# Normalising two row tiles one block product later in a masked attention kernel with a hand-written ScalarE order

## The chip, the core and the metric

The kernel runs on one core of a Trainium2 chip. The core has a matrix engine (TensorE, PE in the profile), a vector engine (VectorE, DVE), an engine for activations and copies (ScalarE, ACT), GpSimd (POOL), and SyncE (SP), which here only issues transfers. Each engine works through its own list of instructions in order and waits at semaphores for the others. The metric is the device time of one execution in microseconds; lower is better. Before the change three executions took 645.16, 645.79 and 647.13 us, median 645.79.

## The reference

One layer of graph attention over 2708 nodes with 1024 features, all in float32:

```
h   = relu(layernorm(x))
q,k,v = h@Wq.T+bq, h@Wk.T+bk, h@Wv.T+bv
z   = (q@k.T)/sqrt(1024) * adj          # adj is 0/1, about 0.15% ones
z   = where(z == 0, -10000, z)
out = x + relu(softmax(z) @ v)
```

A node has some four neighbours, so the kernel finds the few columns of each row of `adj` that are not zero, gathers those rows of `h`, and does the softmax over them alone.

## The kernel before

Rows are worked on in 22 tiles of 128. Wq and Wk are first joined into one matrix M, so that scores are products of `h@M` with gathered rows of `h`; Wv is applied after the softmax. The heavy work is therefore two multiplications of all row tiles by a 1024x1024 matrix. They are done for two tiles at a time (a unit): `("q", 0, 1)`, `("q", 2, 3)`, `("q", 4, 5)`, `("q", 6, 7)` and so on, and later `("o", ...)` units with Wv. A unit is cut into 2x2 blocks of 512 and takes seven block products instead of eight, so it needs sums of blocks of the rows (s1 to s4) and of the matrix (T). A block product is four calls, which the trace shows as eight matmuls of 128x512.

`multiply(n, ...)` writes out one unit. It holds three accumulator banks: X and Z, which start as copies of the bias row (`banks_for`, line 713), and Y, which starts as a copy of X after its first product (line 961). The first two products of the next unit, `a11` into its X and `s1` into its Z, are made inside the current one, by `between(n)`, ahead of the current unit's last product (`a22` into Y). Four banks are shared by all units, so the next unit's Z bank is the one that the current unit's X leaves when `c11` has copied it out (line 1026).

Between the products stand calls `after(i)`, i from 0 to 6. They do what lies beside the multiplication. First come the parts of the next unit: turning its rows with TensorE (line 402, eight transposes of 128x128 for a tile), copies and sums of blocks (lines 684 and 688), and at i = 3 the two bias copies. Then come the steps that the table `steps_at` names for (unit, i):

- `a6`: `apply(6)`, two ScalarE activations (line 263) that normalise the row tiles 6 and 7 in place;
- `k6`: `keep(6, False)`, which stores both to `h_dram` by two transfers from ScalarE's queue (line 270) and leaves their addition to `hsum` for later;
- `p13`, `p14`: `counted(k)`, one ScalarE pass over a tile of `adj` that counts its ones (line 355);
- `f`, `e`, `i`: `found`, four VectorE searches of an `adj` tile for its ones (line 376), and `listed`, which sorts out what was found for a batch of up to four tiles (lines 389 to 395).

The `adj` tiles come through three buffers, `adj_sb[0..2]`. A load into a buffer (line 347, SP's queue) waits until both the count on ScalarE and the search on VectorE have read what is in it.

Up to unit 4 the lists of ScalarE and VectorE stand exactly as the code is written (`manual_schedule`); GpSimd's list is written out for the first part as well. TensorE's and SP's lists are set by a scheduler that takes the data dependences into account. So a step that is moved in the table moves at once on ScalarE, and can move other work on TensorE and SP.

The place in question is in unit 1 (tiles 2 and 3), after its third product (i = 2) and after its fourth (i = 3). The rows of tiles 6 and 7 are named `x_941` and `x_943`; unit 3 turns and multiplies them. In unit 1 the banks are `ps_876` (X), `ps_878` (Z) and a `psy`; unit 2's are `ps_1079` and `ps_1081` before the change, and named `ps_1075` and `ps_1077` after it. Unit 3's X and Z are `ps_1256` and `ps_1258`, its sums `s_1241` (s1), `s_1245` (s2) and so on. The results of unit 1 are `q_990` and `q_991`, stored to `q_dram` from ScalarE's queue (line 1022) behind the copy of line 1037; those of unit 2, `q_1187` and `q_1188`, are stored from SP's queue.

Of the kernel before, what the change touches and what calls it, by code (L numbers as in the profile page):

```python
# [63 lines left out]
def tile_preln_masked_attention(  # L64
# [651 lines left out]
    def natural_rows(n):  # L716
# [16 lines left out]
    nc.vector.tensor_scalar(large[:, 1:2], large[:, 1:2], 250000.0 / D, None, op0=ALU.is_gt)  # L733

    steps_at = {(0, 0): "s4-5 p8 e9 +19 +20 +21", (0, 1): "r4 +0 +1 +2 i10.0-1", (0, 3): "p10", (0, 4): "i10.2-3 a4",
# [4 lines left out]
    steps_ahead = {(1, 5): "o1", (3, 6): "o0"}  # L740
# [740 lines left out]
```

## Time and profile before

| | |
|---|---|
| median of three executions | 645.79 us (645.16 to 647.13) |
| profiled execution | 646.32 us |
| its span, first to last instruction | 644.5 us |
| granted TensorE clock | 0.998 |
| TensorE busy | 636.8 us |
| VectorE busy | 521.3 us |
| GpSimd busy | 376.3 us |
| ScalarE busy | 279.8 us |
| HBM read and written | 159.81 MB, 42.31 MB |

The profile's views used here are: the page (totals by engine and costly groups), the list of waits (who waited for whom), the timeline (instructions in order, with the idle time ahead of each and what ended it in brackets), the chain of waits (the chain of work that ended last, followed back), tables by stretches of time, and the transfers by queue in a stretch. In the timeline an entry begins with its start and its length in us. A queue's name ends in q: `SPq` is SP issuing a transfer. Queue q1 of the transfers carries what SP issues, q10 what ScalarE issues, q0 what GpSimd issues.

### The profile page before, as it was taken

To read this page: it belongs to the slowest core of one execution; us is meant where nothing else is said; L and a number is where in the kernel's file an instruction comes from. 1 tells how busy PE (TensorE), PEld (TensorE's weight loads), DVE (VectorE), ACT (ScalarE), POOL (GpSimd) and SP (SyncE) were. 2 spreads that over 40 slices of the span, in tenths; PEclk is the share of its full clock that TensorE was granted. 3 is DMA by queue.
4 is the path that set the end of the run, shared out by engine and by line. 5 is a ranking of instruction groups with operands and counts; after the bars stand their busy time and mean duration, and the time that the engine had idled before them with its cause. 6 is when DMAs were issued, how large, how long until landed. Compare 5 with 4: busy or idle time off the path is not lost.

```text
span 644.5 us, 6383 instructions
## 1 busy us (share of the span) xinstructions
PE 636.8 (99%) x1731; PEld 326.5 (51%) x1731; DVE 521.3 (81%) x1014; ACT 279.8 (43%) x426; POOL 376.3 (58%) x400
## 2 busy tenths in 40 slices
PE   9999999999999999999999999999999999999996
PEld 5777766444444444445444444454544444545442
DVE  5999789888796765989878959987999999989121
ACT  3448984849586532323133132433333344333300
POOL 2649950975859457744734635565685856762431
PEclk9999999999999999999999999999999999999999
DMA  8999997598699969997877998988798989984542
GB/s 340 407 350 326 345 340 289 203 327 297 226 325 347 382 203 398 374 372 253 319 236 271 420 417 283 334 270 250 248 322 282 288 324 322 306 234 122 147 144 88
DMA packets 61986, 189.02 MB, mean 293 GB/s; under 512 B 10701, under 2 KB 11037, under 8 KB 61048
## 3 DMA queue, kind: packets, MB, share of 16 engines
q0 software_dynamic: 27888, 84.95, 41.1%
q1 hardware_dynamic: 29994, 89.36, 37.6%
q10 hardware_dynamic: 4062, 14.24, 5.7%
q8 instruction: 16, 0.26, 0.2%
q14 instruction: 26, 0.21, 0.1%
HBM read 159.81 MB, written 42.31 MB: 314 GB/s over the span
## 4 chain that ended last, share of the span: by engine, by line
PE 94%; DVE 3%; DMA 2%; issue 0%; POOL 0%; POOLq 0%; SPq 0%
PE ps L948 42%; PE psy L948 30%; PE ps_y L463 6%; PE pt L402 5%; PE ps_x L463 4%; PE ps_z L463 4%; DMA adj<-in_adj_dram 2%; DVE at L376 1%; PE ps_y L498 1%; DVE st L224 1%; PE ps_h L1153 0%; PE ps_v L581 0%; DVE cand L394 0%; DVE sort L668 0%; DVE y_alone L1297 0%
## 5 line engine op out<-in xcount | busy, mean ns | idle before, releaser
L597 POOL DMA_INDIRECT g<-h_dram,tab x105 | 124.4, 1184 | 70.4 <-issue 22.0
L948 PE MATMUL ps<-M,a 128*128 128x512 f32 x320 | 144.1, 593 | 0.6 <-ACT ps L713 0.6
L948 PE MATMUL psy<-wlow,s 128*128 128x512 f32 x320 | 143.9, 592 | 0.0
L826 DVE SCALAR_TENSOR_TENSOR junk<-g,pq 128x1024 uint8<-128x1024 f32 x93 | 114.1, 1227 | 8.3 <-DMA g<-h_dram,tab 5.9
L879 DVE SCALAR_TENSOR_TENSOR u<-g,coef,u 128x1024 f32<-128x1024 f32 x79 | 101.4, 1283 | 5.6 <-ACT u L871 3.7
L948 PEld LDWEIGHTS ps<-M,a 128*128 128x128 f32 x320 | 59.3, 190 | 69.0 <-issue 67.4
L948 PEld LDWEIGHTS psy<-wlow,s 128*128 128x128 f32 x320 | 59.2, 190 | 67.3 <-issue 66.5
L376 DVE FIND_INDEX8 at<-ones,adj 128x8 uint32<-128x685 f32 (+1 forms) x88 | 74.5, 865 | 0.0
L948 PE MATMUL ps<-wlow,s 128*128 128x512 f32 x160 | 72.0, 593 | 0.8 <-DVE s L688 0.8
L948 PE MATMUL psy<-wlow,a 128*128 128x512 f32 x160 | 72.2, 593 | 0.0
L948 PE MATMUL ps<-M,s 128*128 128x512 f32 x160 | 71.9, 592 | 0.0
L355 ACT ACTIVATE sized<-adj 128x2708 uint8<-128x2708 f32 (+1 forms) x22 | 54.2, 2465 | 9.4 <-DMA adj<-in_adj_dram 8.5
L285 POOL TENSOR_TENSOR hsum<-hsum,x 128x256 f32<-128x256 f32 (+1 forms) x56 | 38.7, 727 | 29.7 <-DVE wlow L431 22.2
L1047 POOL DMA_INDIRECT y<-in_x_dram,tab x19 | 32.8, 1726 | 32.5 <-ACT taken L1013 11.2
L948 PEld LDWEIGHTS ps<-wlow,s 128*128 128x128 f32 x160 | 30.3, 190 | 39.3 <-issue 36.4
L948 PEld LDWEIGHTS ps<-M,s 128*128 128x128 f32 x160 | 30.3, 190 | 38.1 <-issue 37.6
L948 PEld LDWEIGHTS psy<-wlow,a 128*128 128x128 f32 x160 | 30.3, 190 | 37.8 <-issue 37.3
L778 POOL DMA_INDIRECT out_dram<-y,tab x21 | 27.8, 1323 | 17.5 <-DMA y<-in_x_dram,tab 9.2
L688 DVE TENSOR_TENSOR s<-a,pt 128x512 f32<-128x512 f32 x40 | 25.6, 682 | 13.1 <-remote 5.9
L684 ACT COPY a<-pt 128x512 f32<-128x512 f32 x60 | 33.4, 589 | 4.6 <-PE psy L948 3.1
L597 POOL DMA_INDIRECT M<-h_dram,tab x20 | 24.9, 1243 | 13.9 <-ACT u L871 4.7
L871 ACT ACTIVATE u<-g,coef 128x1024 f32<-128x1024 f32 x16 | 18.4, 1148 | 25.2 <-DVE m L869 12.3
(238 smaller groups left out, 848.4 us busy)
## 6 DMA issues: line engine op xcount, KB each, us to landing
adj<-in_adj_dram SPq DMA_DIRECT2D x21, 1354.0 KB
x<-in_x_dram SPq DMA_DIRECT2D x21, 512.0 KB
h_dram<-x ACTq DMA_DIRECT2D x21, 512.0 KB
q_late<-q SPq DMA_DIRECT2D x12, 512.0 KB
pq<-q_late SPq DMA_DIRECT2D x12, 512.0 KB
u_dram<-u SPq DMA_DIRECT2D x10, 512.0 KB
or<-u_dram SPq DMA_DIRECT2D x10, 512.0 KB
g<-in_wv_dram SPq DMA_DIRECT2D x16, 256.0 KB
```

Source lines behind the costliest of these rows:

```text
L285: small.append(nc.gpsimd.tensor_add(hsum[:n, cols], hsum[:n, cols], xt[:n, cols]))
L355: nc.scalar.activation(sized[:n], a[:n, :, :PW], AF.Abs, accum_out=total[:n, t:t + 1])
L376: nc.vector.max_index(at[:n, k - first_k, g, :], ones[:n, 0:8], a[:n, g, :])
L402: nc.tensor.transpose(pt[:, c, :], xt[:, k * P:(k + 1) * P], ident)
L463: mm = nc.tensor.matmul(bank, a_tile(o + H * a[0], a[1], i), b(o), start=first and o == 0, stop=(o == H - 1), skip_group_check=True)
L597: return nc.gpsimd.indirect_dma_start(out=dst, out_offset=None, in_=src, in_offset=off, bounds_check=N - 1, oob_is_err=False)
L684: nc.scalar.copy(ops[name], bank)
L778: to = nc.gpsimd.indirect_dma_start(out=out, out_offset=bass.IndirectOffsetOnAxis(ap=ptab.bitcast(U32)[:n, t, SLOTS:SLOTS + 1], axis=0), i ...
L826: chained(lambda: nc.vector.scalar_tensor_tensor(junk, g_of[t][s], 1.0, tq[t], op0=ALU.mult, op1=ALU.mult, accum_out=zall[:, t, s:s + 1]))
L879: chained(lambda: nc.vector.scalar_tensor_tensor(u, g_of[t][s], coef[:, at[t][s]:at[t][s] + 1], u, op0=ALU.mult, op1=ALU.add))
L948: mm = nc.tensor.matmul(bank, a[:, c, :], b[:, c, :], start=False, stop=(c == 3), skip_group_check=True)
L1047: return nc.gpsimd.indirect_dma_start(out=y[:n], out_offset=None, in_=x, in_offset=off, compute_op=ALU.add)
```

## The change

The steps `a6 k6` are taken from place (1, 2) of the table and put at the head of place (1, 3):

```diff
-                (0, 5): "f11 p11 k4 s6-7", (0, 6): "+3 +4 f12 m6 m7", (1, 1): "p12 f13 c1 r6 +5", (1, 2): "p13 a6 k6",
-                (1, 3): "p14", (1, 5): "s8-10 w8-14 r8 w15-21 f14 f15", (1, 6): "f16 p15", (2, 1): "f17",
+                (0, 5): "f11 p11 k4 s6-7", (0, 6): "+3 +4 f12 m6 m7", (1, 1): "p12 f13 c1 r6 +5", (1, 2): "p13",
+                (1, 3): "a6 k6 p14", (1, 5): "s8-10 w8-14 r8 w15-21 f14 f15", (1, 6): "f16 p15", (2, 1): "f17",
```

On ScalarE, in unit 1 between the count of the last 20 rows of `adj` and the count `p14`, the order changes as follows (lines with + stand so after the change, lines with - before it):

```order
 L355 ACTIVATE sized,total<-adj_157 20x2708
+L1026 COPY q_990<-ps_876 128x512
+L713 COPY ps_1075<-bp_sb 128x512
+L713 COPY ps_1077<-bp_sb 128x512
 L263 ACTIVATE x_941<-x_941,r 128x1024
 L263 ACTIVATE x_943<-x_943,r 128x1024
 L270 DMA h_dram<-x_941 128x1024
 L270 DMA h_dram<-x_943 128x1024
-L1026 COPY q_990<-ps_876 128x512
-L713 COPY ps_1079<-bp_sb 128x512
-L713 COPY ps_1081<-bp_sb 128x512
```

The copy of unit 1's X and the two bias copies into unit 2's banks now stand ahead of the two activations and the two stores, instead of behind them.

On TensorE, at the end of unit 1, the scheduler has placed the turning of tile 6 differently:

```order
 L664 MATMUL ps_all<-sort,ones_h 128x252
+L948 MATMUL ps_1075<-M,a_997 128x512 x4
+L948 MATMUL ps_1077<-wlow,s_1060 128x512 x4
+L948 MATMUL psy<-wlow,a_892 128x512 x4
 L402 MATMUL pt<-ident,x_941 128x128 x8
-L948 MATMUL psy<-wlow,a_892 128x512
-L948 MATMUL ps_1079<-M,a_997 128x512 x4
-L948 MATMUL ps_1081<-wlow,s_1060 128x512 x4
-L948 MATMUL psy<-wlow,a_892 128x512 x3
 L948 MATMUL psy<-wlow,s_1064 128x512 x4
```

Before, the transposes of `x_941` and one of the four calls of unit 1's last product stood ahead of unit 2's first two products; now unit 2's two products come first, then unit 1's last product in one piece, and then the transposes.

On SP, one load of `adj` and one store of unit 2 change places, further down:

```order
 L347 DMA adj_155<-in_adj_dram 128x4x677
 L347 DMA adj_157<-in_adj_dram 128x4x677
+L347 DMA adj_159<-in_adj_dram 128x4x677
 L1022 DMA q_dram<-q_1187 128x1024
-L347 DMA adj_159<-in_adj_dram 128x4x677
 L347 DMA adj_155<-in_adj_dram 128x4x677
 L1022 DMA q_dram<-q_1188 128x1024
```

The load into the third `adj` buffer now stands ahead of the store of `q_1187`. VectorE's and GpSimd's lists are the same in both kernels.

## The prediction

> **What bounds the kernel now.** I read the page first, then the list of waits for TensorE, then the timeline around the moved steps, and last the chain of waits through that place.
>
> The page's span and engine totals:
>
> ```profile
> span 644.5 us, 6383 instructions
> PE 636.8 (99%) x1731; PEld 326.5 (51%) x1731; DVE 521.3 (81%) x1014; ACT 279.8 (43%) x426; POOL 376.3 (58%) x400
> ```
>
> TensorE is busy for all but 7.7 us. The list of all its waits (us in total, times, longest):
>
> ```profile
> PE ps_y L498 <- POOL hsum L112: 1.2, 1, 1.2
> PE ps L948 <- DVE s L688: 0.8, 1, 0.8
> PE ps L948 <- ACT ps L713: 0.6, 1, 0.6
> ```
>
> The first is the start of the program; what the list lacks of the 7.7 us, some 5, is the tail behind the last matmul. So two waits are left in the middle, and both lie near the change. Nothing that leaves the matmuls as they are can win much more than these two, while losses have no such bound. TensorE's timeline there (start, length, instruction, idle time before it):
>
> ```profile
> 144.23 3.60 PE L948 MATMUL ps<-M,a 128*128 128x512 f32 x8
> ...
> 154.76 1.04 PE L402 MATMUL pt<-ident,x 128*128 128x128 f32 x8
> 155.63 1.09 PE L948 MATMUL psy<-wlow,a 128*128 128x512 f32 x2
> 157.31 3.70 PE L948 MATMUL ps<-M,a 128*128 128x512 f32 x8 [0.59 <-ACT ps L713]
> 160.85 3.60 PE L948 MATMUL ps<-wlow,s 128*128 128x512 f32 x8
> 164.28 2.74 PE L948 MATMUL psy<-wlow,a 128*128 128x512 f32 x6
> 166.85 3.60 PE L948 MATMUL psy<-wlow,s 128*128 128x512 f32 x8
> ...
> 181.46 3.60 PE L948 MATMUL ps<-M,a 128*128 128x512 f32 x8
> 185.82 3.67 PE L948 MATMUL ps<-wlow,s 128*128 128x512 f32 x8 [0.76 <-DVE s L688]
> 189.33 3.60 PE L948 MATMUL psy<-wlow,a 128*128 128x512 f32 x8
> ```
>
> Ends are modelled, so I go by starts. A group of eight without a stall takes 3.43 us (160.85 to 164.28), that is 0.43 for one matmul, and the eight transposes 0.87 (154.76 to 155.63).
>
> Stall one: from 154.76 to 166.85 TensorE does eight transposes and 24 matmuls, 0.87 + 3 x 3.43 = 11.16 us of work in 12.09. It lost **0.93**.
>
> Stall two: from 181.46 to 189.33 stand two groups, 6.86 in 7.87. It lost **1.01**, waiting for VectorE's sum s1 of unit 3 (`s_1241`).
>
> **Stall one: what ScalarE does there.** ScalarE's timeline:
>
> ```profile
> 153.40 2.36 ACT L263 ACTIVATE x<-x,r 128x1024 f32<-128x1024 f32 x2
> 154.66 1.48 ACTq L270 DMA_DIRECT2D h_dram<-x  x2
> 156.18 0.59 ACT L1026 COPY q<-ps 128x512 f32<-128x512 f32 x1 [0.42 <-PE pt L402]
> 156.66 1.11 ACT L713 COPY ps<-bp_sb 128x512 f32<-128x512 f32 x2
> 167.06 0.59 ACT L1037 COPY q<-psy 128x512 f32<-128x512 f32 x1 [1.99 <-PE psy L948]
> 167.06 0.94 ACTq L1022 DMA_DIRECT2D q_dram<-q  x2
> ```
>
> The bank that `a_997` accumulates into is filled by the first copy of line 713, which stands behind two activations and the issue of two stores: from 153.40 to 156.18, 2.78 us. Those four are what moves. The copy of line 1026 needs the product into unit 1's X, the one at 144.23, so with the four out of the way it starts at 153.40, and the first bank is ready 2.78 earlier: TensorE could begin that group at 157.31 - 2.78 = 154.53. TensorE reaches it at 154.76, as it now stands right behind the small product `ps_all`. Margin 0.23; the whole 0.93 goes. Should the second bank copy hang on VectorE's last read in unit 1, which ends at 155.5 by the chain below, it still has until 154.76 + 3.43 = 158.19.
>
> **The four moved instructions in their new place.** The two activations follow at about 154.9 and end near 157.3, the stores are issued by 157.7, and the count `p14` starts then as before (both orders have the same sum). Three others wait for them. The copy that opens Y of unit 2 (line 961) stands behind `p14` and ends near 161; TensorE wants that bank for s2 at 154.76 + 3 x 3.43 + 0.87 = 165.92, 5 us later. The transposes of tile 6 come at 165.05, 8 us after its activation. The two stores to `h_dram` (0.52 MB each) are issued about 2.5 us later. What hides them is the quiet stretch of the transfer engines, in the table by stretches (busy time of each engine, clock, share of the transfer engines, GB/s):
>
> ```profile
> 163.00:167.00 4.00, 4.00 (x11) 1.85 (x10) 4.00 (x10) 0.59 (x1) 2.97 (x4) 1.00 0.07 14
> ```
>
> 0.07 busy for 4 us: a megabyte that slips 2.5 us runs into an empty stretch. Cost 0; without that cover, up to 2.6 us of delay for the load below.
>
> **Stall two: what is late there.** Taking 0.93 out ahead would by itself make TensorE wait 0.93 longer at 185.82, if `s_1241` comes no earlier. So the forecast hangs on what holds VectorE. The chain of waits through it:
>
> ```profile
> 154.85 0.69 DVE q L1029
> ...
> 162.98 3.39 DVE at L376 x4
> ...
> 166.43 10.14 DMA adj<-in_adj_dram
> ...
> 178.40 3.48 DVE at L376 x5
> ...
> 185.01 0.68 DVE s L688
> ```
>
> VectorE's last search of the batch waits for a load of `adj` issued at 166.43, by SP, when the buffer came free; the load takes 12 us until 178.40. VectorE had nothing to do from 173.08 on:
>
> ```profile
> 172.22 0.86 DVE L376 FIND_INDEX8 at<-ones,adj 128x8 uint32<-128x685 f32 x1
> 178.40 0.09 DVE L376 MATCH_VALUE_LOAD at<-ones,adj 128x8 f32 x1 [5.31 <-issue]
> ```
>
> Why 12 us for 1.39 MB (128 x 2708 x 4 bytes)? The transfers by queue (packets, MB, share), first row from 166.4 to 171, the next two from 171 to 175.7:
>
> ```profile
> q1 hardware_dynamic: 195, 0.53, 49.4%
> ...
> q10 hardware_dynamic: 259, 0.98, 53.5%
> q1 hardware_dynamic: 313, 0.84, 45.4%
> ```
>
> From 171 on, the load (q1) shares the engines half and half with the two stores of unit 1 (q10, 2 x 0.52 MB), issued at 167.06, just behind it. Now these stores move. They are issued with the copy of line 1037, which waits for unit 1's last product. That ended at 166.85 (the copy began 0.21 later); with the three groups in a row from 154.76 it ends at 165.05, so copy and first store come at 165.26, 1.17 **ahead** of the load, the second store 0.61 later. The load's own issue hangs on VectorE's searches since 154.85, behind a product ahead of the change, and stays at 166.43.
>
> What is a store worth that is issued ahead of the load? Behind the load, those of 167.06 moved nothing by 171 (no q10 in the first row). One that no load preceded closely is that of 183.26, with the q10 row from 184 to 185:
>
> ```profile
> 183.26 0.34 ACTq L270 DMA_DIRECT2D h_dram<-x  x1
> ...
> q10 hardware_dynamic: 89, 0.36, 91.8%
> ```
>
> It ran at full rate within 1 us. I take this case, as the engines are as empty at 165 as they were then. The stores then run from about 166.2, and 1.05 MB at the (0.98 + 0.84) / 4.7 = 0.39 MB/us of the shared rows end near 168.9, when the load begins to move. By 171 it has its 0.53 MB less at most 0.1; the other 0.9 to 1.0 take 2.5 us, to 173.5. The last confirmation came 178.40 - 175.7 = 2.7 later than the load's 1.39 MB were through; I keep between 0.3 and that, so 173.8 to 176.2, where VectorE has waited until 178.40. `s_1241`, now at 185.69, comes 2.2 to 4.6 earlier, at 183.5 at the latest. TensorE, 0.93 early, asks for it at 184.89 - 0.93 = 183.96. The stall goes whole, 1.01. The point from which it does not: the load landing after 176.6.
>
> The Trainium skill (DMA: Bandwidth & Descriptors, section "Latency and other measured facts") puts the first byte of such a transfer at about 0.6 us. The trace agrees at 183.26 and not at 167.06, where it was over 3.9; by that figure the stores would start at 165.9, which is on the side of the sum.
>
> The load that SP now issues ahead of the store of `q_1187` stood behind it until 188.72:
>
> ```profile
> 188.72 4.07 SPq L347 DMA_DIRECT2D adj<-in_adj_dram  x2
> ```
>
> It can go once its buffer is read, by 182. It feeds searches after 190, on an engine that TensorE does not wait for there. I cost it at 0; the cover is that no wait of TensorE's list lies behind 189.33. The store loses nothing: its data come later than that load's issue.
>
> **Sum.** 0.93 + 1.01 = 1.94 us. The profiled execution, 646.32 (span 644.5 and 1.8 around it), becomes 644.38; the median, 645.79, which is 0.53 below it, becomes 643.85. I write 643.9, for a few hundredths lost in new small waits.
>
> **Rivals.**
>
> *The second stall swallows the first.* The four microseconds before a ScalarE store moves may be its own and not due to the load ahead. Then the stores start at 169.3 instead of 171.1, share with the load from its beginning, and the load's end is set by the same 2.4 MB. It lands at most 0.3 earlier; TensorE waits 1.6 at `s_1241`. Total -0.1 to -0.4: 645.5. For it: both rows of 171 to 175.7 are at the engines' full rate. Against: 183.26. A rule of the Trainium skill stands on its side (same page, "Issuing engines are not separate DMA queues"): transfers from different engines run on the same 16 engines and interleave whoever issued them. By that rule the order of issue alone would not free the load. The q10 rows agree from 171 on, but not before, where one queue ran alone.
>
> *A new wait on ScalarE.* Ahead of unit 3's copy into Y (line 961) stand two counts, and TensorE wants that bank at its next s2:
>
> ```profile
> 178.02 0.59 ACT L1026 COPY q<-ps 128x512 f32<-128x512 f32 x1 [3.02 <-remote]
> 190.96 0.58 ACT L961 COPY psy<-ps 128x512 f32<-128x512 f32 x1
> 192.76 3.60 PE L948 MATMUL psy<-wlow,s 128*128 128x512 f32 x8
> ```
>
> The copy ends at 191.54; TensorE, 1.94 early, asks at 190.82. If ScalarE does not move, 0.72 is lost: 644.6. ScalarE is packed from 178.02 on, where it was let go by something that the row does not name; if that is TensorE or a transfer, it moves too, which I hold likelier.
>
> *Slower.* Unit 4's rows are gathered by GpSimd and turned by TensorE:
>
> ```profile
> 194.65 1.07 POOL L599 DMA_INDIRECT qr<-h_dram,tab  x1 [0.17 <-issue]
> 203.06 1.04 PE L402 MATMUL pt<-ident,qr 128*128 128x128 f32 x8
> ```
>
> TensorE did not wait at 203.06, so the gather was there after at most 8.4 us. With 1.94 gained it is wanted at 201.12, and the loads of weights that follow the search on SP are pulled forward against it. Landing after 203.06 makes the kernel slower, after 205.0 by over 0.3%; a gather a third longer than 8.4 us lands at 205.9, 2.8 above before: 648.6. Against: the pulled-forward `adj` load leaves that stretch, and GpSimd's work ahead of the gather hangs on VectorE, which is early.
>
> *Nothing happens*, because something else holds the bank copies: 645.8. The 0.42 ahead of line 1026 is the stores' issue, so I see nothing that would.
>
> **How the numbers follow.** Both stalls gone 0.68; the second swallows the first 0.12; ScalarE's wait 0.08; slower 0.11; nothing 0.01. The bound between change and no change is 0.3% or 1.94 us, about what a measurement of this kernel can tell, and the likeliest case sits on it: I split its 0.68 into 0.38 beyond and 0.30 within, since nearly all of the middle idle time would have to go and it cannot be exceeded by much. Faster 0.38; same 0.30 + 0.12 + 0.08 + 0.01 = 0.51; slower 0.11. The likeliest case's own range is 643.3 to 644.6, the spread of the three runs below the median (0.6) on either side. The range takes in ScalarE's wait and the swallowed stall: 643.3 to 645.8, which leaves out the slower case and a little below.
>
> **What would show it.** In the changed profile: `a_997`'s product starting at 154.8 with no idle time; the stores of line 1022 at 165.3, ahead of the load at 166.4; q10 empty by 170; VectorE's fourth search in a row with less than 3 us of idle time instead of 5.31; no VectorE wait in TensorE's list; TensorE busy for all but some 6 us, span 642.6. Wrong would be: a wait of TensorE on line 688 of 1 us or more (the swallowed stall), on line 961 (ScalarE), on the rows `qr` (slower), or any wait over 0.3 us behind 190 that is not there now.

## The result and the profile after

The changed kernel takes 644.24 us (median of 22 executions, 643.61 to 644.88). The kernel before, on the same chip, takes 645.76 (22 executions, 643.82 to 647.13). The ratio is 0.9979, with a 95% interval of 0.9973 to 0.9986: a gain of 0.21%, clear of the noise and within the 0.3% that counts as "same". The medians lie 1.52 us apart. The forecast was 643.9, with "same" the likeliest of the three.

The profiled execution of the changed kernel took 643.61 us. The page's span and engine totals, answering to those of before (644.5 and 636.8):

```profile
span 641.9 us, 6381 instructions
PE 635.2 (99%) x1731; PEld 326.2 (51%) x1731; DVE 521.9 (81%) x1014; ACT 279.6 (44%) x426; POOL 377.3 (59%) x400
```

The list of all waits of TensorE (us in total, times, longest):

```profile
PE ps_y L498 <- POOL hsum L112: 1.2, 1, 1.2
PE ps_x L463 <- DMA wlow<-in_wq_dram: 0.3, 1, 0.3
```

The two waits in the middle are gone. What is left lies in the first microseconds of the program. TensorE's timeline through the changed place (start, length, instruction):

```profile
153.94 0.27 PE L664 MATMUL ps_all<-sort,ones_h 128*128 128x252 bf16 x1
154.04 3.60 PE L948 MATMUL ps<-M,a 128*128 128x512 f32 x8
157.48 3.60 PE L948 MATMUL ps<-wlow,s 128*128 128x512 f32 x8
160.91 3.60 PE L948 MATMUL psy<-wlow,a 128*128 128x512 f32 x8
...
179.83 3.60 PE L948 MATMUL ps<-M,a 128*128 128x512 f32 x8
183.26 3.60 PE L948 MATMUL ps<-wlow,s 128*128 128x512 f32 x8
186.70 3.60 PE L948 MATMUL psy<-wlow,a 128*128 128x512 f32 x8
```

No row has a bracket. Unit 2's first group starts 0.10 behind `ps_all`, and the group on `s_1241` (183.26) follows its predecessor after 3.43 us, a group without a stall.

A ruler for all kernels below is the time from the start of `ps_all` to the start of unit 3's group `psy<-wlow,a`, since the work between them is the same everywhere and the variation of the program's first 154 us is left out. After the change it is 186.70 - 153.94 = 32.76. Before, `ps_all` stood at

```profile
154.65 0.27 PE L664 MATMUL ps_all<-sort,ones_h 128*128 128x252 bf16 x1
```

and the other group at 189.33, so 34.68. The difference is **1.92**; the forecast's sum was 1.94. The spans differ by 2.6, because this execution of the changed kernel also reached the place 0.7 earlier.

On ScalarE the copies now come first, and the stores of line 1022 are issued at 164.55:

```profile
152.62 0.56 ACT L1026 COPY q<-ps 128x512 f32<-128x512 f32 x1
153.08 1.09 ACT L713 COPY ps<-bp_sb 128x512 f32<-128x512 f32 x2
154.12 2.37 ACT L263 ACTIVATE x<-x,r 128x1024 f32<-128x1024 f32 x2
155.39 1.48 ACTq L270 DMA_DIRECT2D h_dram<-x  x2
...
164.55 0.95 ACTq L1022 DMA_DIRECT2D q_dram<-q  x2
```

SP issues the load of `adj` at 165.69 (165.69 - 164.55 = 1.14 behind the first store), and VectorE's fourth search in a row finds it at 174.24:

```profile
165.69 12.63 SPq L347 DMA_DIRECT2D adj<-in_adj_dram  x4
```

```profile
174.24 0.09 DVE L376 MATCH_VALUE_LOAD at<-ones,adj 128x8 f32 x1 [1.89 <-DMA adj<-in_adj_dram]
```

Before, this row stood at 178.40 with 5.31 us of idle time. Counted from `ps_all`, the load is there after 20.30 us instead of 23.75. The transfers by queue (packets, MB, share of the 16 engines) from 165 to 167, the next two rows from 167 to 169, and the last from 169 to 171:

```profile
q10 hardware_dynamic: 174, 0.65, 83.6%
...
q10 hardware_dynamic: 114, 0.40, 67.8%
q1 hardware_dynamic: 49, 0.13, 25.0%
...
q1 hardware_dynamic: 229, 0.62, 97.3%
```

The stores (q10) run alone first, then the load (q1) runs alone. Before, the load began alone and then shared the engines half and half.

### The profile page after: what moved, and what is told of

It reads as the page before. It is cut to its first block, busy times and chain, and to the rows that moved or that the text cites. A ratio compares the mean times of both kernels' runs of the same rounds, so it can differ in the third digit from the quotient of the medians.

```text
span 641.9 us, 6381 instructions
## 1 busy us (share of the span) xinstructions
PE 635.2 (99%) x1731; PEld 326.2 (51%) x1731; DVE 521.9 (81%) x1014; ACT 279.6 (44%) x426; POOL 377.3 (59%) x400
## 4 chain that ended last, share of the span: by engine, by line
PE 98%; DMA 1%; DVE 0%; POOL 0%; POOLq 0%; issue 0%
PE ps L948 45%; PE psy L948 32%; PE ps_y L463 6%; PE pt L402 6%; PE ps_x L463 4%; PE ps_z L463 4%; DMA wlow<-in_wq_dram 1%; PE ps_h L1153 0%; PE ps_v L581 0%; DVE y_alone L1297 0%; POOL out_dram L1281 0%; POOLq L1303 0%; PE ps_all L664 0%; PE ps_in L662 0%; PE ps_b L728 0%
```

## The experiments

All comparisons are with the kernel before, run on the same chip beside each of them. The first two tried to set the place of the stores by the order of the code alone.

**Stores behind an extra pass (changed kernel).** One more ScalarE pass stands between the copy of line 1037 and unit 1's two stores:

```diff
             nc.scalar.copy(qb[:, lo], Y)
+            if ta == 2:
+                pause = work.tile([P, D], mybir.dt.uint8, tag="junk", name="junk_p", bufs=1)
+                nc.scalar.activation(pause, bp_sb, AF.Copy)
             if ta < EARLY:
```

> The changed kernel with one more ScalarE pass of about 1.1 us (a copy of the bias rows into a scratch tile) between unit 1's last copy and its two stores, so that the stores are issued some 0.4 us behind the load of adj instead of 1.1 us ahead of it. Nothing else moves. Theory (the second stall went because the stores are ahead of the load): the stores move nothing for some 4 us, then share the engines with the load, VectorE's fourth search starts near 177.5 on the changed kernel's clock instead of 174.2, and TensorE waits 1 to 2 us on line 688. Time 645.2 to 646.0, as before the change. Rival (the load is quick in the changed kernel for another reason, such as the later stores to h_dram or the scheduler's new order on TensorE): the search starts at 174 to 174.5, TensorE has no wait there, 644.2.

Measured: 643.86 (11 executions), ratio 0.9979 (0.9970 to 0.9987), as the changed kernel. The edit did not do what it was meant to. ScalarE's timeline, and SP's row:

```profile
165.39 0.33 ACTq L1022 DMA_DIRECT2D q_dram<-q  x1
165.86 1.06 ACT L1040 ACTIVATE junk_p<-bp_sb 128x1024 uint8<-128x1024 f32 x1
166.00 0.33 ACTq L1022 DMA_DIRECT2D q_dram<-q  x1
```

```profile
166.56 7.76 SPq L347 DMA_DIRECT2D adj<-in_adj_dram  x3
```

Both stores stand behind the pass in the list, and were issued at 165.39 and 166.00, before it and in the midst of it, since they use nothing that it writes. They were still ahead of the load, so the run does not test the theory. It shows two other things. One more pass of 1.06 us on ScalarE costs nothing here by itself. And something else moved that the expectation left out: the scheduler put SP's list back to that of the kernel before (the store of unit 2 at 185.28, the `adj` load behind it at 185.71), and the gain is whole without SP's swap.

**Stores behind the next count (kernel before).** The stores are written after the count `p15`:

```diff
+    postponed = []
...
+            if ta == 2:
+                postponed.append(lambda: (store(qa, ta), store(qb, tb)))
+                return
...
+            if (n, i) == (1, 6):
+                postponed.pop()()
```

> The kernel before, with unit 1's two stores held back until after the next count of adj on ScalarE, some 3 us later, so that they are issued some 4 us behind the load that VectorE waits for. The order of the bank copies is as before. Theory: the load no longer shares the engines, VectorE's wait of 5.31 us shrinks to under 2, the wait of TensorE on line 688 (1.01 with its slow start) goes, the wait on line 713 (0.93) stays: 645.76 - 1.0 = 644.8. Rival (the load is slow on its own account): nothing changes, 645.8.

Measured: 645.83 (11 executions), ratio 1.001 (1.000 to 1.002). The same happened: the stores were issued at 166.60, before the count began (166.96), and at 167.10, while it ran. Both came right behind the load of 166.30, as in the kernel before. Both waits of TensorE stayed. Inconclusive too.

**Only the stores to `h_dram` moved (kernel before).** The activations stay ahead of the copies, so that TensorE's and SP's lists are those of before:

```diff
-  (1, 2): "p13 a6 k6", (1, 3): "p14",
+  (1, 2): "p13 a6", (1, 3): "k6 p14",
```

> The kernel before, with only the two stores to h_dram moved behind the bank copies, the two activations left ahead of them. The copies come about 0.5 us earlier instead of 2.8. TensorE's list stays as before. The first stall shrinks from 0.93 to about 0.4. Unit 1's stores are issued near 166.5, still not ahead of the load at 166.4. Theory: the second stall takes what the first gives, 645.5 to 645.8. Rival (every tenth that ScalarE gives back is kept): 645.76 - 0.5 = 645.2.

Measured: 644.56 (12 executions), ratio 0.9988 (0.9979 to 0.9996). In this execution the two stores of unit 1 straddled the load: the first was issued at 165.59, the load at 165.78, the second store at 166.20. The load was then found at

```profile
176.53 0.09 DVE L376 MATCH_VALUE_LOAD at<-ones,adj 128x8 f32 x1 [4.10 <-DMA adj<-in_adj_dram]
```

With no store ahead VectorE waits 5.31, with one 4.10, with both 1.89. TensorE's wait on line 688 shrank to 0.36. Neither branch of the expectation holds, since the time is below the 645.2 of the rival: stall one was all but gone (the group behind the bank copies started at 155.94, where the matmuls ahead of it left off at 155.88 by their starts), and a part of stall two went too, which the expectation had not seen coming.

**Stores forced behind the load (changed kernel).** This time the first result is rewritten in place, so that the stores depend on the pass:

```diff
             nc.scalar.copy(qb[:, lo], Y)
+            if ta == 2:
+                nc.scalar.copy(qa, qa)
             if ta < EARLY:
```

> The changed kernel with one more pass of ScalarE (about 1.1 us) that rewrites the first result of unit 1 in place between the copy of line 1037 and the two stores, so that the stores depend on it and cannot be issued before about 166.3 and 166.9, some 0.6 to 1.2 us behind the load of adj at about 165.7 instead of 1.1 and 0.5 ahead of it. The bank copies stay first. My theory (the place of the stores in the order of issue decides when the load lands): q10 starts over 2.5 us after the first store's issue instead of 0.8, the load lands at 177 or later, VectorE's fourth search waits 4.5 us or more instead of 1.9, the wait for the bank copies stays away, and TensorE waits 1.2 to 2.0 us for the sum of line 688: 645.0 to 646.0, that is 0.9 to 1.9 above the changed kernel of the same call, about the kernel before. Rival (the order of the stores is not what freed the load; the whole gain comes from the bank copies): no wait on line 688 over 0.3, within 0.4 us of the changed kernel.

Measured: 645.99 (12 executions), ratio 1.0008 (0.9996 to 1.0019); the changed kernel beside it took 644.41, so 1.58 is lost. The rows of SP, ScalarE's queue, VectorE, and the list of waits:

```profile
165.73 4.48 SPq L347 DMA_DIRECT2D adj<-in_adj_dram  x2
```

```profile
166.16 0.88 ACTq L1022 DMA_DIRECT2D q_dram<-q  x2
```

```profile
177.94 0.09 DVE L376 MATCH_VALUE_LOAD at<-ones,adj 128x8 f32 x1 [5.55 <-DMA adj<-in_adj_dram]
```

```profile
PE ps L948 <- DVE s L688: 1.9, 1, 1.9
PE ps_y L498 <- POOL hsum L112: 1.2, 1, 1.2
PE pt L402 <- DMA qr<-h_dram,tab: 0.2, 1, 0.2
```

The load and the first store are 0.43 us apart, in the order of before; the wait for the bank copies is gone, and the whole gain is gone with it. TensorE merely waits 1.9 in one place instead of some 1 in each of two. The transfers from 169 to 171:

```profile
q1 hardware_dynamic: 165, 0.45, 60.2%
q10 hardware_dynamic: 73, 0.30, 36.3%
```

From 167 to 169 there was no q10 at all; once it runs, it shares. SP's list is again that of the kernel before, as with the extra pass above. These two runs are therefore the closest pair: the same list on SP and a pass of 1.05 or 1.06 us more on ScalarE in both, the stores ahead of the load in one and behind it in the other. TensorE loses nothing in the first and waits 1.9 on line 688 in the second.

**Stores forced far behind (kernel before).** As the second experiment, but with the dependent pass:

```diff
-                postponed.append(lambda: (store(qa, ta), store(qb, tb)))
+                postponed.append(lambda: (nc.scalar.copy(qa, qa), store(qa, ta), store(qb, tb)))
```

> The kernel before with its order of bank copies, activations and stores to h_dram; only unit 1's two stores to q_dram are put off: they stand behind the count p15 and behind a pass (about 1.1 us) that rewrites the first of the two results in place, so that they depend on it and are issued at about 170 to 172, when the load of adj issued at about 166.5 has had the engines for itself. My theory: the load lands by 174, VectorE's fourth search waits less than 2.5 us instead of 5.3, TensorE no longer waits for the sum of line 688; the wait for the bank copies, 0.93 lost, stays: 0.7 to 1.1 us below the kernel before. Rival (the load is late whatever the stores do): VectorE waits 5 us as before, TensorE about 0.8 to 1.1 on line 688, no change of time beyond 0.3 us.

Measured: 645.42 (12 executions), ratio 1.0001 (0.999 to 1.0013). The profile and the median disagree. In the profile the stores were issued at 170.34, VectorE waited 0.57, TensorE did not wait on line 688, and it reached unit 3's group 32.99 after `ps_all`, 1.69 less than before; of this it lost 0.72 again at the rows `qr` of unit 4. The median moved by 0.1. So it was run again:

> The kernel with unit 1's two stores put off by the dependent pass, once more, since its profile (1.0 less from ps_all to the end) and its median (0.1 less) did not agree. If the profile was right: median 0.6 to 1.0 below the kernel before, wait on qr 0.3 to 0.6. If the median was right: a longer wait on qr in this profile, 0.8 or more, because the put-off stores push the stores to h_dram behind them, on which the gather of qr waits; median within 0.3.

Measured: 644.56 (12 executions), ratio 0.9989 (0.9979 to 0.9999). The list of waits of this profile:

```profile
PE pt L402 <- DMA qr<-h_dram,tab: 1.6, 1, 1.6
PE ps_y L498 <- POOL hsum L112: 1.2, 1, 1.2
```

Neither branch of the expectation holds, since the median is low and the wait on `qr` is long. GpSimd stood idle ahead of the gather of these rows:

```profile
194.56 1.07 POOL L599 DMA_INDIRECT qr<-h_dram,tab  x1 [3.49 <-PE psy L948]
```

The row names a matmul. The transfers issued from 182 to 190 (KB, us from issue to landing) point elsewhere:

```profile
h_dram<-x ACTq DMA_DIRECT2D x1, 512.0 KB, 8.1
tab<-tab_dram POOLq DMA_DIRECT2D x1, 117.0 KB, 10.1
tab<-tab_dram POOLq DMA_DIRECT2D x1, 1.4 KB, 9.0
```

The last store to `h_dram`, issued at 182.36, landed at 190.5. The two loads of `tab`, the table of row numbers that the gather reads, were issued at 183.65 and 184.95 and landed at 193.8 and 194.0, and the gather followed some 0.6 later. The first execution agrees (`tab` at 193.2 and 193.5, the gather at 194.02). So by the traces it was the table that came late, and not a store to `h_dram`, as the expectation had it; no run tests this alone. What is settled is that stall two goes when the stores are far behind, and that the gain can be lost again at `qr`. The two medians (645.42 and 644.56) differ by as much as the effect, so no size is taken from them.

**Stores forced ahead (kernel before).** Both stores are issued ahead of the copy of line 1037. The kernel leaves out the second tile's rows in the second store, which carries the first tile's once more:

```diff
         def c21(Y):
+            if ta == 2:
+                store(qa, ta)
+                store(qa, tb)
+                nc.scalar.copy(qb[:, lo], Y)
+                return
             nc.scalar.copy(qb[:, lo], Y)
```

> The kernel before, bank copies, activations and stores to h_dram as they were; unit 1's two stores to q_dram are issued ahead of the copy of line 1037 (about 164 and 164.6) instead of behind it (167.1, 167.7). The result of the second tile is not complete by then, so the second store carries the rows of the first tile once more: same size, same rows of q_dram, other data. My theory: both stores have run by 168.5, the load of adj issued at about 166.5 has the engines for itself, VectorE's fourth search waits 1.5 to 3 us instead of 5.3, TensorE's wait on line 688 (1.0) goes, the wait for the bank copies (0.5 to 0.9, as far as ScalarE's start varies) stays; nothing is pushed later, unlike where the stores are put off. From the small product ps_all to the end 0.8 to 1.1 us less than in the kernel before (489.9), and 0.6 to 1.2 us less by the medians. Rival (stall two alone is worth nothing, because the gathered rows qr of unit 4 are then waited for by as much): a wait of TensorE on qr of 0.6 or more, median within 0.3 of before.

Measured: 644.97 (12 executions), ratio 0.999 (0.998 to 1.0), 0.52 below before and short of the 0.6 expected at least; the interval reaches 1.0, so the median alone does not show the gain. The profile is as expected; the stores, the load, the search, and the waits:

```profile
164.46 0.82 ACTq L1022 DMA_DIRECT2D q_dram<-q  x2
```

```profile
166.96 0.54 SPq L347 DMA_DIRECT2D adj<-in_adj_dram  x1
```

```profile
175.95 0.09 DVE L376 MATCH_VALUE_LOAD at<-ones,adj 128x8 f32 x1 [2.34 <-DMA adj<-in_adj_dram]
```

```profile
PE ps_y L498 <- POOL hsum L112: 1.2, 1, 1.2
PE ps L948 <- ACT ps L713: 0.6, 1, 0.6
PE ps_in L662 <- DVE sort L650: 0.3, 1, 0.3
PE ps_x L463 <- DMA wlow<-in_wq_dram: 0.3, 1, 0.3
```

Line 688 is not in the list any more, line 713 still is: stall two goes by the order of the stores alone, with the bank copies where they were.

**The changed kernel again, and the kernel before again.**

> The changed kernel once more, on the same chip as the others, as their yardstick and as a second profile. My theory: 1.3 to 1.9 us below the kernel before, no wait of TensorE on lines 688 and 713, VectorE's fourth search waits 1.7 to 2.5 us. If the profile of the changed kernel was a lucky one: a wait on line 688 of 0.3 us or more.

Measured: 644.41 (12 executions), ratio 0.9986 (0.9974 to 0.9997), 1.12 below the kernel before, where 1.3 to 1.9 were expected. The profile is as expected: the ruler gives 32.76 once more, with no wait on lines 688 and 713, and VectorE's fourth search waits 1.75. The kernel before was profiled a second time:

> The kernel before once more, to see how far its two stalls differ from one execution to the next. If the second hangs on how a load and two stores share the engines, it varies by several tenths, since the time of the last of the load's parts does; the first, which is ScalarE's order alone, stays at 0.9 within 0.1.

It took 647.38, with a span of 645.7. Its list of waits:

```profile
PE ps_y L498 <- POOL hsum L112: 1.2, 1, 1.2
PE ps L948 <- DVE s L688: 1.1, 1, 1.1
PE ps L948 <- ACT ps L713: 0.7, 1, 0.7
PE pt L402 <- DMA qr<-h_dram,tab: 0.4, 1, 0.4
PE ps_in L662 <- DVE sort L650: 0.3, 1, 0.3
```

By starts, as in the forecast, stall one is 1.01 here (0.93 in the first profile) and stall two 1.39 (1.01). Both are as this expectation had them, but the table shows stall one much smaller in other executions of the same order.

**All profiles on one ruler.** "Load found" is the start of VectorE's fourth search after `ps_all`. "Lost" is the ruler's stretch less 32.76. "At `qr`" is what TensorE lost at unit 4's rows by starts: from the group before them to the transposes, less 3.43. Times in us.

| kernel | stores against the load | load found | stretch | lost | at `qr` |
|---|---|---|---|---|---|
| before | behind | 23.75 | 34.68 | 1.92 | 0 |
| before, again | behind | 24.47 | 35.41 | 2.65 | 0.59 |
| before, behind the next count | behind | 24.09 | 35.02 | 2.26 | 0 |
| changed, forced behind | behind | 23.95 | 34.88 | 2.12 | 0.36 |
| before, only `h_dram` stores moved | one ahead | 22.49 | 33.43 | 0.67 | 0.43 |
| before, forced ahead | ahead | 21.38 | 33.73 | 0.97 | 0 |
| before, forced far behind | far behind | 18.99 | 32.99 | 0.23 | 0.72 |
| the same, again | far behind | 18.88 | 32.90 | 0.14 | 1.77 |
| changed | ahead | 20.30 | 32.76 | 0 | 0 |
| changed, again | ahead | 20.15 | 32.76 | 0 | 0 |
| changed, extra pass | ahead | 20.62 | 32.76 | 0 | 0 |

The first five rows follow one line: what is lost is "load found" less 21.82, within 0.02 us, whether the bank copies come first (fourth row) or not. Below 21.82 the load costs nothing, and only the bank copies are left: 0.97 where they are late, 0.14 and 0.23 in the two executions in which ScalarE happened to run further ahead of TensorE (its count of the last 20 rows of `adj` began 4.4 and 4.5 us before `ps_all`, against 3.4 to 3.7 in the other four with the order of before), nothing where they come first. This lead is set earlier. In all eleven profiles that count began 9.12 to 9.14 us after the pass of line 233, at 140.38 to 141.99, which had waited 1.2 to 2.8 us for a load of `x`. The size of stall one therefore hangs on when that load lands, and is not ScalarE's order alone. So the two stalls are not two prices that can be had one by one. The late load sets the sum, and stall one is a part of it that is only seen once the load is early. One change alone gives nothing (copies first, load late: 2.12 lost, against 1.92) or half (load early, copies late: 0.97; more where ScalarE is early); both gave all of it in three profiles out of three.

## Why the prediction was right

- *Stall one.* `a_997`'s group was to start right behind `ps_all` with no idle time: 154.04 behind 153.94. Right. The copy of line 1026 starts 0.8 earlier than the forecast's 153.40, of which 0.7 is the execution's earlier start.
- *The four moved instructions at no cost.* Right: the activations ran from 154.12, the count behind them from 156.91, line 961 at 159.38, and no one waited. The stores to `h_dram` were put off by 1.4 us and not by 2.5 (155.39 against 154.66, with the 0.7 put back).
- *The stores ahead of the load.* Forecast 1.17 ahead, measured 1.14. Their packets were to be done by 168.9 to 170: q10 has no row in 169 to 171. The load was to be found at 173.8 to 176.2; it was found at 174.24, which is 174.95 with the 0.7 put back. VectorE's idle time was to be below 3: 1.89. Where the forecast lets the trace agree at 183.26 on the first byte, it agrees only roughly: the first packet came 0.84 us after the issue there, and 0.85 after that of 164.55.
- *Stall two.* Right, with the condition that the forecast set (landing by 176.6, that is 21.95 after `ps_all`; the table has 21.82).
- *SP's swap at no cost.* Right for the time, not for the way: the load that stood behind the store of `q_1187` at 188.72 is issued at 177.78, the store itself at 184.07, and TensorE waits for nothing behind. But the load now stands 2.17 us ahead of the next stores to `h_dram`. The first of these was issued at 179.95 and moved nothing before 183.90; the three took 8.4 us to land (median), against 3.5 with the extra pass, where the load stands behind the store. The gather of `qr`, which needs them, was issued 38.76 us after `ps_all`, against 36.85 there. The swap put the gather off by some 2 us, as far as this pair of runs tells, and slack hid it.
- *The second stall swallows the first* was the rival to fear, and what it feared is real: with the stores forced behind the load, the changed kernel loses all it gained. The cause that it supposed is not: a delay of the stores' own of some 4 us would have been there with the stores ahead too, and it was 0.85. It did not happen here because 1.14 us of order were enough. The rule of the Trainium skill (DMA: Bandwidth & Descriptors, "Issuing engines are not separate DMA queues"), that transfers interleave whichever engine issued them, holds once both queues run (36.3% and 60.2% above). The conclusion drawn from it for this rival, that the order of issue would not free the load, fell: 0.43 us behind or 1.14 ahead made 3.65 us for the load's landing (23.95 and 20.30).
- *ScalarE's wait at line 961.* Did not come: ScalarE moved by more than TensorE, the copy ran at 187.65 where it was at 190.96, and TensorE wanted it at 190.13 where it was 192.76.
- *Slower through `qr`.* Did not come in the two profiles of the changed kernel, yet it was nearer than the forecast's argument said. That held that GpSimd's gather hangs on VectorE, which is early. In the changed kernel the gather waits for a store to `h_dram` instead:

```profile
192.70 1.07 POOL L599 DMA_INDIRECT qr<-h_dram,tab  x1 [2.38 <-DMA h_dram<-x]
```

It was issued 192.70 - 153.94 = 38.76 after `ps_all`, where the kernel before had 40.00, so TensorE's gain of 1.92 left it 0.7 less time, and it still sufficed. With the stores far behind it did not (0.72 and 1.77 lost). There was some luck in it: from the gather's issue to the transposes the two profiles of the changed kernel had 7.73 and 8.22 us, and in the five executions in which TensorE waited for these rows the same way took 7.84 to 9.02.
- *The size.* The sum was 1.94 and the ruler shows 1.92. The medians show 1.52. The forecast subtracted a sum made in one execution from the median of others; the losses of the kernel before differ between executions (1.92 and 2.65 + 0.59 in its two profiles), so one profile did not give the mean. Stall one alone was between 0.14 and 1.01 in executions with the bank copies last, as the landing of `x` fell. That the other executions of before lose less than the profiled one fits the medians, but was not seen in a trace of that kernel. TensorE's idle time fell from 7.7 to 6.7 us, not to some 6: its modelled busy time counts a part of the stalls as work (33.33 of the 34.68 us before, where 32.76 is the work).
- *"Same".* The forecast's sum lay on the bound of 0.3%, and "same" came out ahead by adding the rivals to a part of the likeliest case. That the medians fell within the bound says nothing for the mechanism; the ruler does.

## What to carry to other kernels

When two transfers from different queues meet, look at which of them is issued first: a microsecond of order decided here who had the engines, and moving copies on one engine changed it on another. Stalls that lie one behind the other on the same engine are not added up before asking what sets the end of the last one: run the early cure and the late cure alone, and both. To put a transfer later in an experiment, make its data late; moving its line behind unrelated work did not hold it back.

## What the runs showed that was not expected

- A store that no load closely precedes begins to move 0.85 us after its issue (164.55 to the first q10 packet at 165.40 in the changed kernel, 0.84 at 183.26 before, 0.83 in the split case). One issued just behind an `adj` load takes 2.8 to 4.1: 166.16 to 169.45 forced behind, 166.20 to 169.02 for the second store of the split case, 167.06 to 171.16 before, 169.63 to 172.67 in the second run far behind, where another load had been issued at 169.11. Loads show the same: the one that the searches wait for takes 1.32 us from its issue to its first packet before (166.43 to 167.75), and 2.76 behind the two stores in the changed kernel (165.69 to 168.45). In these rows the transfer that is issued second starts late, whichever it is; why it does not share from its start is not shown.
- A transfer of ScalarE's queue is issued while an earlier, unrelated pass of ScalarE still runs (166.00, with the pass from 165.86 to 166.92), or before it has begun (165.39). That an engine works through its list in order holds for its passes, not for the transfers among them.
- TensorE, whose list does not differ up to there, reached the same matmul, `ps_all`, between 153.91 and 154.77 us in these profiles; one kernel's two profiles are 0.18 apart. Of a span's difference, up to 0.86 lay ahead of the place that was changed.
